# Giving VectorE's steps from a head pair's sums to their reciprocals a high scheduling rank in a masked attention kernel

## The chip, the cores and the metric

The kernel runs on one core of a Trainium2 chip. The metric is the device time of one execution in microseconds (us), the median of several runs. A profile is one more execution, taken by the hardware profiler.

## What is computed

The reference is one attention layer with a residual, over 16 batches of 1024 tokens with 512 channels and 8 heads of 64. The same projection serves as query, key and value. The mask is 0 or 1 per token.

```python
xt = jnp.transpose(x, (0, 2, 1))
q = xt @ Wq.T
qh = q.reshape(B, T, NH, dk).transpose(0, 2, 1, 3)
scores = scale * jnp.einsum('bhqd,bhkd->bhqk', qh, qh)
logits = (scores * cmask + (1.0 - cmask) * NEG) * rmask
attn = jax.nn.softmax(logits, axis=-1)
ctx = jnp.einsum('bhqk,bhkd->bhqd', attn, qh)
out = ctx.transpose(0, 2, 1, 3).reshape(B, T, D) @ Wo.T
return x + jnp.transpose(out, (0, 2, 1))
```

A token whose mask is 0 attends to every token alike, so its row of the result is a mean. About half of the tokens have mask 1.

## The kernel before, in words

The kernel gathers the tokens with mask 1 of a batch into 544 slots (C), 512 of them in four tiles of 128 and a tail of 32 (CT), and does the attention over these alone. The other tokens get the mean's projection, added by their own path (L798). Slots beyond the number of kept tokens hold the mean too; what they add to a softmax sum is worked out (corr, L571 and L572) and subtracted.

The work of one batch b goes through 18 steps, in a list S. A pair p is two heads (p is 0 to 3). For a pair and a tile i of 128 slots, `scores` computes the logits of both heads on TensorE (L620, into the two buffers of the psum pool pss), and ScalarE takes the exponential (L624), which also writes the sum over a row into z. Two further steps do the 32 slots of the tail for four heads at once, a group g (pairs 0 and 1 are group 0, pairs 2 and 3 group 1): the matmuls L595, the exponential L599 with its sums into zt, then on VectorE a split of the result into a high and a low part (L604 and L605), and four transfers on SP's queue that lay these parts out as pt (L611 from L604's result, L612 from L605's). Of pt, the first L611 and the first L612 serve the even pair of the group, the others the odd pair.

`attend` multiplies the exponentials by the values: 32 matmul records of L643 for a pair's tile, accumulating in pav, and four of L647 for the tail, which read pt. ScalarE copies pav out (L651).

The sums become reciprocals in `recip_sums`, the function that is changed. Its VectorE steps are: L666 subtracts corr from the eight sums z of a pair; L671 does the same for the tail's sums, once per head, between partitions of different groups (it reads zt and corr at partitions 32 q and writes partitions 0 to 31); L672 clamps and scales; L673 takes the reciprocal; L674 multiplies by the mask hit of valid slots. All write rcol, of which there are two tiles, one for even pairs and one for odd ones. Then `recip_rows` transposes rcol on TensorE (L680), copies ten rows out on VectorE (L683, which already has the high rank), sends them to memory and back spread over partitions (rd L685 and rb L688, on SP). `norm` multiplies the copied-out pav by rb (L711) and splits it for the output projection (L712 to L717), whose matmuls are L727 and whose eviction, with the residual, is L732. Its results go out with indirect transfers on GpSimd's queue (L811).

Between these steps stands the work for the next batches: gathering (L339), transposes (L424) and their splits (L384, L385), the query projection L447 with its eviction L450 and L453 and its split into hl (L461 to L463, then transfers into xx), the values (L497, L500, L484, L485), range checks (L392, needed only at the end), loads of 512 KB of x for the means (xm, L374), and the row maxima that bound the exponent: L541 and L543 gather squares into smcol, L549 transposes them on TensorE, L551 takes the maximum m, L558 spreads it on TensorE, and L560 to L563 make nm from it. All psum tiles but pss and pav come from the pool pm, of two buffers.

What sets the order: `run` lists the calls batch by batch, with a cost for each, and deals them out over the steps. A scheduler then orders the instructions of each engine. It takes them by rank, which is the place in the program; `high_priority(offset=HPO)`, with HPO = 300, moves the rank of what is issued inside it 300 places forward. Before the change it stands around the splits L384 and L385, the first L643 of a group, L683, L732 and the first row maxima. Each engine then executes its queue strictly in that order, with semaphores for what it needs from the others. `behind` and `once` add order by hand; L711 waits for TensorE's progress that way (for pairs 0 to 2).

Of the kernel before, what the change touches and what calls it, by code (L numbers as in the profile page):

```python
# [15 lines left out]
ALU = mybir.AluOpType  # L16
# [3 lines left out]
P = 128  # L20
# [11 lines left out]
CT = C - 512  # L32
# [3 lines left out]
HG = H // 2  # L36
# [6 lines left out]
SX = 256.0  # L43
# [3 lines left out]
HPO = 300  # L47


class Fast:  # L50
# [608 lines left out]
    def recip_sums(self, b, p):  # L659

        nc, s = self.nc, self.st[b]
        hs, g = slice(2 * p, 2 * p + 2), p // 2
        corr = s["corr"][g]
        r = self.rcol[p % 2][:, :10]
        m = r.rearrange("p (h k) -> p h k", k=5)
        nc.vector.tensor_tensor(m[:, :, :4], s["z"][:, hs, :],  # L666
                                corr[:, p % 2 * 2:p % 2 * 2 + 2].unsqueeze(2).broadcast_to([P, 2, 4]), ALU.subtract)
        for h in range(2):
            q = (2 * p + h) % HG
            rows = slice(q * CT, (q + 1) * CT)  # L670
            nc.vector.tensor_tensor(m[:CT, h, 4:5], s["zt"][rows, g:g + 1], corr[rows, HG:], ALU.subtract)  # L671
        nc.vector.tensor_scalar(r, r, 1e-35, 1.0 / SX, ALU.max, ALU.mult)  # L672
        nc.vector.reciprocal(r, r)  # L673
        nc.vector.tensor_tensor(m, m, self.hit[:, b, :].unsqueeze(1).broadcast_to([P, 2, 5]), ALU.mult)  # L674

    def recip_rows(self, b, p):

# [532 lines left out]
```

## Time and profile before

| | us |
|---|---|
| median of 3 runs | 1070.85 (1070.66 to 1076.17) |
| the profiled execution | 1064.91 |
| its span, first to last instruction | 1063.1 |
| TensorE busy (PE) | 1021.6 |
| VectorE busy (DVE) | 729.2 |
| ScalarE busy (ACT) | 672.5 |
| GpSimd busy (POOL) | 298.6 |
| the lines of recip_sums on VectorE, busy | 10.5 (L666), 19.0 (L671), 11.3 (L672), 13.5 (L673), 10.7 (L674) |
| TensorE idle before L680, waiting for L674 | 6.3, in 9 waits |

How to read it: PE is TensorE's matmuls and PEld its weight loads, which overlap them. The mean granted clock of TensorE was 0.992. A row of a timeline has the start in us, the duration of a run of equal instructions, engine, line, operation, result and operands, shape, and in brackets how long the engine had been idle and what ended that. A row of the view of waits has who waited, for whom, and then us in total, number of waits and the longest. Matmuls are pipelined: rows of them overlap, and one that takes 0.28 us holds the engine for about 0.12.

### The profile page before, as it was taken

Reading aid. Unit: us, or ns where it says so; the run is one execution under the profiler, and the core shown is the slowest. Engines: PE = TensorE matmul, PEld = TensorE weight load, DVE = VectorE, ACT = ScalarE, POOL = GpSimd, SP = SyncE. Lnnn points to the kernel's source line nnn. Section 1 sums busy time; section 2 is a strip of 40 time slices with the busy share of each in tenths; the row PEclk is TensorE's granted clock in tenths of the full one; section 3 lists DMA queues with packets and bytes.
Section 4 is the critical chain, followed back from the end, with each engine's and each line's share of the span. In section 5 each row is a group of like instructions: output and inputs, shape, how many; then the busy total and the mean of one; then the engine's idle time right before and its main releaser. Section 6 shows DMA issues by size and latency. Waiting matters only on the chain.

```text
span 1063.1 us, 23765 instructions
## 1 busy us (share of the span) xinstructions
PE 1021.6 (96%) x8626; PEld 701.6 (66%) x8626; DVE 729.2 (69%) x2376; ACT 672.5 (63%) x1722; POOL 298.6 (28%) x303
## 2 busy tenths in 40 slices
PE   7798999999999999999999999999999999999996
PEld 7576666666666767666676666767666676766553
DVE  6697668676766856776775766876676776666653
ACT  5876666666676766666676576676666676664550
POOL 3101013322301222332322223232232332235652
PEclk9899999999999999999999999999999999999998
DMA  6746555546654665766557575655856554575752
GB/s 206 226 132 166 136 166 165 177 142 204 174 145 137 160 189 156 195 194 165 173 149 210 167 199 172 162 166 148 239 174 179 170 159 144 142 195 170 222 172 76
DMA packets 78123, 181.37 MB, mean 171 GB/s; under 512 B 15008, under 2 KB 16800, under 8 KB 78000
## 3 DMA queue, kind: packets, MB, share of 16 engines
q1 hardware_dynamic: 56816, 111.62, 38.4%
q0 software_dynamic: 21184, 68.18, 20.5%
q8 instruction: 70, 1.15, 0.5%
q14 instruction: 53, 0.43, 0.1%
HBM read 92.34 MB, written 33.91 MB: 119 GB/s over the span
## 4 chain that ended last, share of the span: by engine, by line
PE 76%; ACT 10%; DVE 7%; issue 3%; DMA 2%; POOL 0%; POOLq 0%; DVEq 0%; SPq 0%; ACTq 0%
PE pav L643 22%; PE pss L620 17%; PE pm L727 15%; PE pm L447 12%; ACT p L624 5%; PE pm L424 2%; PE pav L647 2%; ACT xh L384 1%; DVE p L605 1%; ACT xm L369 1%; PE pss L595 1%; PE pm L497 1%; PE pm L680 1%; ACT v L500 1%; ACT p L599 1%
## 5 line engine op out<-in xcount | busy, mean ns | idle before, releaser
L624 ACT ACTIVATE p<-pss,nm 128x544 f32<-128x544 f32 x512 | 365.4, 718 | 217.5 <-PE pss L620 203.6
L620 PE MATMUL pss<-xx 128*128 128x272 f16 x2048 | 307.0, 280 | 6.5 <-ACT p L624 5.7
L643 PE MATMUL pav<-p,v 128*64 128x272 f32 x2048 | 248.8, 396 | 0.0
L620 PEld LDWEIGHTS <-xx 128*128 128x128 f16 x2048 | 194.7, 99 | 63.3 <-issue 22.5
L643 PEld LDWEIGHTS pav<-p,v 128*64 128x64 f32 x2048 | 141.4, 137 | 91.0 <-issue 13.9
L811 POOL DMA_INDIRECT y_out<-xa,idx x68 | 72.1, 1060 | 292.8 <-PE pss L620 150.2
L447 PE MATMUL pm<-xh,wqh 128*128 128x274 f16 (+1 forms) x512 | 143.9, 281 | 2.4 <-DVE xa L732 1.9
L447 PE MATMUL pm<-xh,wql 128*128 128x274 f16 (+1 forms) x512 | 143.2, 280 | 0.0
L447 PE MATMUL pm<-xl,wqh 128*128 128x274 f16 (+1 forms) x512 | 143.1, 280 | 0.0
L339 POOL DMA_INDIRECT xa<-x_in,idx x68 | 67.9, 999 | 210.6 <-PE pss L620 101.5
L447 PEld LDWEIGHTS <-wqh 128*128 128x128 f16 x1024 | 98.1, 99 | 25.8 <-issue 4.8
L624 ACT ACTIVATION_READ_ACCUMULATOR p<-pss,nm 128x1 f32 x512 | 104.0, 203 | 0.0
L811 POOL DMA_INDIRECT y_out<-xi,idx x60 | 69.5, 1159 | 107.5 <-PE pss L620 49.0
L727 PE MATMUL pm<-woh,ch 128*128 128x512 f16 x240 | 91.1, 380 | 0.0
L727 PE MATMUL pm<-woh,cl 128*128 128x512 f16 x240 | 90.9, 379 | 0.0
L727 PE MATMUL pm<-wol,ch 128*128 128x512 f16 x240 | 90.9, 379 | 0.0
L450 ACT ACTIVATE q<-pm 128x272 f32<-128x272 f32 (+1 forms) x128 | 50.9, 398 | 63.0 <-PE pm L447 62.8
L339 POOL DMA_INDIRECT xi<-x_in,idx x60 | 61.4, 1023 | 102.2 <-PE pss L620 43.5
L732 DVE SCALAR_TENSOR_TENSOR xa<-pm,xa 128x512 f32<-128x512 f32 x60 | 41.3, 688 | 63.3 <-PE pm L727 59.9
L727 PEld LDWEIGHTS <-ch 128*128 128x128 f16 x480 | 45.6, 98 | 45.9 <-issue 1.4
L798 DVE TENSOR_TENSOR xi<-xi,ub 128x512 f32<-128x512 f32 (+1 forms) x60 | 40.9, 688 | 42.6 <-PE pss L620 42.0
L711 DVE TENSOR_TENSOR c<-c,rb 128x544 f32<-128x544 f32 x64 | 46.2, 722 | 28.0 <-PE pm L447 17.1
(194 smaller groups left out, 1558.4 us busy)
## 6 DMA issues: line engine op xcount, KB each, us to landing
xx<-hl SPq DMA_DIRECT2D x256, 136.0 KB
xm<-x_nat_in SPq DMA_DIRECT2D x56, 512.0 KB
rb<-rd SPq DMA_DIRECT2D x128, 136.0 KB
pt<-c SPq DMA_DIRECT2D x64, 136.0 KB
pt<-p SPq DMA_DIRECT2D x64, 136.0 KB
ub<-ud SPq DMA_DIRECT2D x16, 256.0 KB
xi<-x_nat_in SPq DMA_DIRECT2D x8, 256.0 KB
xa<-x_in,idx POOLq DMA_INDIRECT x68, 4.6
```

The costliest lines, as they stand in the source:

```text
L339: dma = self.nc.gpsimd.indirect_dma_start(out=tile[:n], out_offset=None, in_=self.x, in_offset=bass.IndirectOffsetOnAxis(ap=idx, axis=0))
L424: self.pe = nc.tensor.transpose(pt[:, c, :], x[:n, c * P:(c + 1) * P], self.ident[:n, :n]).ins
L447: self.beat = nc.tensor.matmul(pq, lhsT=w[:, c, e * P:(e + 1) * P], rhs=xx[:, c, cols], start=(k == 0), stop=(k == 3 * DC - 1)).ins
L450: nc.scalar.activation(s["q"][:, e, cols], pq, AF.Copy, scale=1.0 / (SX * SW))
L620: self.beat = nc.tensor.matmul(pt[:, g, :CH], lhsT=xx[:, 2 * k, i * P:(i + 1) * P], rhs=xx[:, 2 * k + a, g * CH:(g + 1) * CH], start=(a == ...
L624: self.exp = [nc.scalar.activation(t.rearrange("p (g c) -> p g c", g=2), pt[:, :, :CH], AF.Exp, bias=s["nm"][p // HG][:, p % HG:p % HG + 1 ...
L643: mm = nc.tensor.matmul(s["pav"][k * DK:(k + 1) * DK, g, :CH], lhsT=s["v"][p][:, i, k * DK:(k + 1) * DK], rhs=ps[k][:, cols], start=(i == ...
L711: self.once(nc.vector.tensor_tensor(c, c, s["rb"][p], ALU.mult), self.beat if p < 3 else None)
L727: nc.tensor.matmul(po[:cols.stop - cols.start], lhsT=a[:, e, cols], rhs=w[:, e, :], start=(e == 0 and k == 0), stop=(e == DC - 1 and k == 2))
L732: self.nc.vector.scalar_tensor_tensor(x, po, 1.0 / (SX * SW), x, ALU.mult, ALU.add)
L798: self.once(self.nc.vector.tensor_tensor(x[:n], x[:n], s["ub"][:n], ALU.add), self.beat)
L811: dma = self.nc.gpsimd.indirect_dma_start(out=self.out, out_offset=bass.IndirectOffsetOnAxis(ap=idx, axis=0), in_=x, in_offset=None)
```

## The change

The body of `recip_sums` from the choice of rcol's tile on is put inside `with self.tc.high_priority(offset=HPO)`. No instruction, tile, shape or transfer is added or removed; the line numbers behind it grow by one.

```diff
@@ -661,17 +661,18 @@
         nc, s = self.nc, self.st[b]
         hs, g = slice(2 * p, 2 * p + 2), p // 2
         corr = s["corr"][g]
-        r = self.rcol[p % 2][:, :10]
-        m = r.rearrange("p (h k) -> p h k", k=5)
-        nc.vector.tensor_tensor(m[:, :, :4], s["z"][:, hs, :],
-                                corr[:, p % 2 * 2:p % 2 * 2 + 2].unsqueeze(2).broadcast_to([P, 2, 4]), ALU.subtract)
-        for h in range(2):
-            q = (2 * p + h) % HG
-            rows = slice(q * CT, (q + 1) * CT)
-            nc.vector.tensor_tensor(m[:CT, h, 4:5], s["zt"][rows, g:g + 1], corr[rows, HG:], ALU.subtract)
-        nc.vector.tensor_scalar(r, r, 1e-35, 1.0 / SX, ALU.max, ALU.mult)
-        nc.vector.reciprocal(r, r)
-        nc.vector.tensor_tensor(m, m, self.hit[:, b, :].unsqueeze(1).broadcast_to([P, 2, 5]), ALU.mult)
+        with self.tc.high_priority(offset=HPO):
+            r = self.rcol[p % 2][:, :10]
+            m = r.rearrange("p (h k) -> p h k", k=5)
+            nc.vector.tensor_tensor(m[:, :, :4], s["z"][:, hs, :],
+                                    corr[:, p % 2 * 2:p % 2 * 2 + 2].unsqueeze(2).broadcast_to([P, 2, 4]), ALU.subtract)
+            for h in range(2):
+                q = (2 * p + h) % HG
+                rows = slice(q * CT, (q + 1) * CT)
+                nc.vector.tensor_tensor(m[:CT, h, 4:5], s["zt"][rows, g:g + 1], corr[rows, HG:], ALU.subtract)
+            nc.vector.tensor_scalar(r, r, 1e-35, 1.0 / SX, ALU.max, ALU.mult)
+            nc.vector.reciprocal(r, r)
+            nc.vector.tensor_tensor(m, m, self.hit[:, b, :].unsqueeze(1).broadcast_to([P, 2, 5]), ALU.mult)
```

## The prediction, made before the changed kernel ran

> **What bounds the kernel.** I read the page first: TensorE is busy for 96% of the span and holds three quarters of the chain that ended last, and VectorE holds 7% of it.
>
> ```profile
> PE 1021.6 (96%) x8626; PEld 701.6 (66%) x8626; DVE 729.2 (69%) x2376; ACT 672.5 (63%) x1722; POOL 298.6 (28%) x303
> ...
> PE 76%; ACT 10%; DVE 7%; issue 3%; DMA 2%; POOL 0%; POOLq 0%; DVEq 0%; SPq 0%; ACTq 0%
> ```
>
> So an edit of VectorE's order counts only where TensorE stands idle for VectorE, or comes to. TensorE's queue is in order, so each such wait is paid in full. The view of waits, TensorE's own, has these rows (us in total, times, longest); its gaps over 0.06 us sum to 32.5 us, 10.8 of them in the first 41 us:
>
> ```profile
> PE pm L680 <- DVE rcol L674: 6.3, 9, 0.7
> PE pss L620 <- ACT p L624: 5.7, 13, 0.7
> ...
> PE pav L647 <- DMA pt<-p: 2.4, 1, 2.4
> ...
> PE pm L447 <- DVE xa L732: 1.9, 5, 0.4
> PE pm L558 <- DVE m L551: 1.1, 5, 0.2
> ...
> PE pm L680 <- ACT p L624: 0.7, 1, 0.7
> ```
>
> The chain of the change ends in the first and the last row: the transpose L680 waits ten times, always for pair 2, in batches 1, 3, 4, 6, 7, 9, 10, 12, 13 and 14. For the other 54 pairs L680 came 0.3 to 7.1 us after L674, or with no gap: there an earlier reciprocal buys nothing. **The most the change can remove is 6.9 us**, plus the 1.9 us of the L447 row if VectorE's eviction L732 came earlier.
>
> One such place on VectorE's timeline (start, us, ...), batch 3, and TensorE's wait at it:
>
> ```profile
> 272.18 0.48 DVE L604 CAST c<-p 128x544 fp32r<-128x544 f32 x1 [0.33 <-ACT p L599]
> 272.58 0.30 DVE L671 TENSOR_TENSOR rcol<-zt,corr 32x1 f32<-32x1 f32 x2
> 272.92 0.72 DVE L605 TENSOR_TENSOR p<-p,c 128x544 fp32r<-128x544 f32 x1
> 273.56 0.17 DVE L672 TENSOR_SCALAR rcol<-rcol 128x10 f32<-128x10 f32 x1
> 273.76 0.31 DVE L671 TENSOR_TENSOR rcol<-zt,corr 32x1 f32<-32x1 f32 x2
> 274.10 0.22 DVE L673 RECIPROCAL rcol<-rcol 128x10 f32<-128x10 f32 x1
> 274.35 0.17 DVE L674 TENSOR_TENSOR rcol<-rcol,hit 128x10 f32<-128x10 f32 x1
> ```
> ```profile
> 274.67 0.30 PE L680 MATMUL pm<-ident,rcol 128*128 128x128 f32 x1 [0.70 <-DVE rcol L674]
> ```
>
> The chain cannot start when the exponentials of the pair are done (269.18): L671 needs the tail's sums, which ScalarE's L599 delivers at 272.15, and L604 needs the same tile.
>
> **The change, part by part.** No instruction is added or removed. The rank goes to the scheduler that writes the queues, so I read the order of the built programs. GpSimd's is the same. 508 rows of VectorE's order move. TensorE's differs in 41 places, all small. On SP the transfers pt (from L604 and L605) and the 512 KB loads xm (L374) change places. Pitch of VectorE, from its timeline: an independent instruction starts 0.08 us before the one ahead ends, a dependent one 0.03 us after; L671 lasts 0.148 us, and what follows it starts 0.014 us after its end. So four L671 in a row hold the queue for 0.066 + 3 x 0.162 + 0.096 = 0.65 us (the first overlaps; the follower doesn't).
>
> A rule on this: the Trainium skill, "VectorE: DVE Perf Modes", section "Two Vector instructions with no wait between them", says an instruction is held until all earlier ones end when its input starts in another group of 32 partitions than the last one's. L671 reads a new group each time, so it speaks against pulling these steps forward; without it the four would take 0.27 us by the pitch of the other rows, and part 2 below would cost 1.3 us and not 3.1. The row decides, and it shows the hold.
>
> 1. *The ten waits.* New order in the nine batches: four L671, L672, L604, L673, L605, L674. The scheduler leaves L604 and L605 inside the chain. From 272.18: L671 to 272.83, L672 to 273.0, L604 from 272.9, L673 from 273.3, L605 from 273.4, L674 ends at 274.2 instead of 274.52. **Gain 9 x 0.31 = 2.8 us**, not 6.3: 0.4 us of each wait stays.
>
> 2. *Group 0 in batches 2, 5, 8, 11, 14.* There the four L671 (for pairs 0 and 1) now stand ahead of L485, where VectorE has no idle time until L551; before, they came some 7 us later and nobody waited. In batch 5:
>
> ```profile
> 359.55 0.68 DVE L485 TENSOR_REDUCE sd<-tmp 128x8 f32<-128x512 f32 x1
> 360.14 0.43 DVE L604 CAST c<-p 128x544 fp32r<-128x544 f32 x1
> ...
> 361.83 0.16 DVE L543 TENSOR_TENSOR smcol<-smcol,sdt 128x4 f32<-128x4 f32 x1
> ...
> 362.77 0.28 DVE L551 TENSOR_REDUCE m<-pm 128x1 f32<-128x128 f32 x1
> ```
> ```profile
> 362.24 0.27 PE L549 MATMUL pm<-ident,smcol 128*128 128x128 f32 x1
> ...
> 363.20 0.35 PE L558 MATMUL pm<-ident,m 128*128 128x4 f32 x2 [0.22 <-DVE m L551]
> ```
>
> L543 ended at 361.99, 0.25 us before L549; L558 waits for L551 already. A shift of 0.65 us goes through to L558 nearly whole. **Loss 5 x 0.62 = 3.1 us.** This is what is queued behind the new early steps, and TensorE waits for it.
>
> 3. *Group 0 in batches 3, 4, 6, 7, 9, 10, 12, 13.* Two L671 were ahead of L551 already, now four: L551 is 0.33 us later. L558 follows it directly (239.04 + 0.28, then 239.40). The new order of TensorE puts one matmul of L620 (0.12 us) ahead of L558. **Loss 8 x 0.21 = 1.7 us.**
>
> 4. *Group 1 in batches 2, 5, 8, 11.* L732 comes 0.43 us later, and TensorE's order now has the 32 matmuls of L643 (3.8 us) ahead of the L447 that waited 0.38 us for it: gain 4 x 0.38 = 1.5. L647 then stands 0.85 us earlier (0.38, and four L620 of 0.47 put behind it), and pt's first half landed 0.45, 1.6, 1.8 and 0.63 us ahead of it: new waits of 0.4 and 0.2 us. SP issues these pt late anyway (210.97, after xx), so L604's shift is hidden. **Gain 0.9 us.**
>
> 5. *Batch 14.* The chain and two hl steps now stand ahead of L543, which comes 2.1 us later, so L549 starts at 969.4 instead of 968.55. L680 moves ahead of twelve L447 and waits for the psum buffer that L551 frees, at about 971.75. From there: L447 1.4 us, L620 0.94, so L643 starts at 974.2 instead of 973.09; the two waits below are in that already. **Loss 1.1 us.**
>
> ```profile
> 969.73 0.28 PE L447 MATMUL pm<-xh,wqh 128*128 128x272 f16 x1 [0.45 <-DVE xa L732]
> ...
> 972.83 0.33 PE L680 MATMUL pm<-ident,rcol 128*128 128x128 f32 x1 [0.63 <-DVE rcol L674]
> ```
>
> 6. *Batch 0.* L605 ends 0.45 us later, and with it pt; TensorE waits for that pt already (2.39 us, at 88.60). **Loss 0.4 us.**
>
> 7. *SP.* In six batches (3, 6, 7, 9, 10, 12) xm is now issued ahead of pt. Cost between nothing and 2.4 us each (batch 0's wait, where xm went first too). I take nothing: in batch 4 xm went first already (335.16, pt from 335.79), pt's first half landed at 341.25 and L647 read it at 343.80, 2.5 us of cover; without that cover the delay would be paid whole. In eight batches xm is issued some 2 us later; ScalarE reads it much later, and no row shows ScalarE waiting for it.
>
> Sum: -2.8 + 3.1 + 1.7 - 0.9 + 1.1 + 0.4 = **+2.6 us** on the profiled execution (1064.91 us with a span of 1063.1), so 1067.5. That execution was 5.9 us under the median of the runs shown, 1070.85; carried over, **1073.5 us**. ScalarE is 0.3 to 0.7 us late at some L571 (it waits for L563), where TensorE is late by as much; I add nothing.
>
> **Rivals.** (A) *Faster:* the rank clears all ten waits and L732's: 6.9 + 1.9 = 8.8 us less, 1062. For it, the view of waits; against it, L604 and L605 still stand inside the chain, and parts 2 and 3. (B) *Slower, by pt:* at L647 of pair 2 in the six batches of part 7. Cover there was 1.7 to 4.2 us; PE arrives 0.3 us earlier and L605 is 0.45 us later, so a landing more than 0.9 to 3.4 us later decides. At batch 0's price, 6 x 2.4 = 14 us more: 1088, and half of it 1081. (C) *Nothing of note:* VectorE is off the path, the small shifts vanish in slack I misjudged: 1070.9. (D) *The losses stand, the gains don't* (the waits at L680 stay 0.7 because the psum buffer or ScalarE holds them): 2.6 + 3.7 gives 1077.
>
> **How the numbers follow.** Forecast 0.55, C 0.2, D 0.12, B 0.09, A 0.04. The measurement tells apart about 0.5% (5.4 us). Faster by more: A, 0.04. Slower by more: B, most of D, and the upper edge of the forecast, 0.2. The rest, 0.76, is within. The range takes in the forecast, C and D, with 3 to 4 us at either end for the spread of the runs (1070.66 to 1076.17), and leaves out A and most of B: 1067 to 1080.
>
> **What would show it.** The row L680 <- L674 at about 3.6 us in 9 waits of 0.4; the row L558 <- L551 up from 1.1 to about 5 (with some at L549 <- L543); no L447 <- L732; small new waits at L647 near 217 and 788; TensorE's gaps from 32.5 to about 35. Wrong if L680 doesn't wait at all, if L549 and L558 don't wait in group 0, or if L647 waits in the six batches.

## The result and the profile after

The changed kernel takes 1075.64 us (median of 20 runs, 1072.36 to 1079.56), the kernel before 1071.06 us beside it (20 runs, 1068.24 to 1076.17): a ratio of **1.0041, 95% interval 1.0032 to 1.0051**, so 4.6 us slower, where 1073.5 us, 2.6 more than before, was forecast. The profiled execution took 1075.52 us with a span of 1073.8. That is 10.6 us more than before's profiled one (1064.91), which was 6 us below its own median; the two traces differ by more than the change makes, and its share has to be told from the rest.

From L666 on, lines of the changed kernel are one higher: L680 is L681, L671 is L672, L674 is L675, L711 is L712, L727 is L728, L732 is L733. The page after, its busy times and its chain:

```profile
PE 1025.3 (95%) x8626; PEld 700.7 (65%) x8626; DVE 722.9 (67%) x2376; ACT 672.2 (63%) x1722; POOL 301.5 (28%) x303
...
PE 71%; DVE 11%; ACT 7%; DMA 5%; issue 4%; SPq 1%; POOL 0%; POOLq 0%; DVEq 0%; ACTq 0%
```

VectorE is busy 6 us less, and its share of the chain rises from 7% to 11%: it is not the amount of its work that counts but where TensorE waits for it. TensorE's waits after (us in total, times, longest):

```profile
PE pm L681 <- DVE rcol L675: 4.5, 9, 0.5
...
PE pav L647 <- DMA pt<-p: 3.3, 5, 1.1
...
PE pm L549 <- DVE smcol L543: 2.7, 6, 0.6
...
PE pm L447 <- DVE nm L560: 2.1, 3, 1.3
...
PE pm L558 <- DVE m L551: 1.8, 7, 0.6
```

The waits that the change is about have shrunk from 7.0 us in ten (6.3 in nine, and 0.7 in the row that the view puts down to ScalarE) to 4.5 us in nine. The row of L447 waiting for L732 is gone. New are 2.5 us at L549, 1.7 at L447 for nm (L560) and 0.7 at L558. For pt there are four new waits of 0.3 to 1.1 us, 2.6 in all, while the one of batch 0 is 0.7 us here and was 2.4 in before.

**How the time was placed.** I took the start of the same matmul in two traces and subtracted. From the transpose L680 of batch 1's pair 1 to that of batch 14's pair 3 (135.77 to 989.67 us in before) this difference changes only at a few matmuls, at most of them by the same amount in each profile; two profiles of before differ by 0.29 us over this stage, three of the changed kernel by 2.5. Outside of it the thirteen profiles differ by up to 8.5 us ahead of the stage and 4.9 behind it, and not in step with the change: no_tail comes to the stage 6.3 us later than before, cast_6_10 1.5 us earlier. Of the 10.7 us between the spans of after and before, 0.7 lie ahead of the stage, 8.1 in it and 1.9 behind it. The stage, in us against the first profile of before, split by the parts of the prediction (a minus is a gain; a2 and a3 are two more profiles of the changed kernel; the other columns are experiments told below):

| part | forecast | after | a2 | a3 | group0 | group1 | flat |
|---|---|---|---|---|---|---|---|
| 1, nine waits at L680 | -2.8 | -1.9 | -1.8 | -1.8 | 0 | -1.8 | -6.0 |
| 2, group 0, five batches | +3.1 | +3.9 | +3.9 | +3.9 | +3.9 | 0 | +1.7 |
| 3, group 0, eight batches | +1.7 | +4.4 | +4.2 | +4.4 | +4.0 | +0.1 | +1.1 |
| 4, group 1, batches 2, 5, 8, 11 | -0.9 | +0.1 | -1.1 | -1.2 | 0 | -0.8 | -0.4 |
| 5, batch 14 | +1.1 | +0.6 | -0.1 | -0.1 | +0.2 | -0.1 | -0.7 |
| 7, pt in batch 3 | 0 | +1.1 | +0.6 | +0.6 | 0 | 0 | +1.5 |
| whole stage | +2.2 | +8.1 | +5.7 | +5.6 | +8.0 | -1.7 | -2.9 |

(Part 6, 0.4 us in batch 0, lies ahead of the stage, where the scatter hides it. The rows are rounded and leave out up to 0.9 us at other matmuls, most of it group1's 0.74 in batch 2.) The three profiles of the changed kernel agree to 0.2 us in parts 1, 2 and 3; nearly all their disagreement is in parts 4, 5 and 7, at waits for transfers.

### The profile page after: what moved, and what is told of

It reads as the page before. It is cut to its first block, busy times and chain, and to the rows that moved or that the text cites. A ratio compares the mean times of both kernels' runs of the same rounds, so it can differ in the third digit from the quotient of the medians.

```text
span 1073.8 us, 23792 instructions
## 1 busy us (share of the span) xinstructions
PE 1025.3 (95%) x8626; PEld 700.7 (65%) x8626; DVE 722.9 (67%) x2376; ACT 672.2 (63%) x1722; POOL 301.5 (28%) x303
## 4 chain that ended last, share of the span: by engine, by line
PE 71%; DVE 11%; ACT 7%; DMA 5%; issue 4%; SPq 1%; POOL 0%; POOLq 0%; DVEq 0%; ACTq 0%
PE pav L643 20%; PE pss L620 16%; PE pm L728 15%; PE pm L447 10%; ACT p L624 3%; DMA pt<-p 2%; PE pav L647 2%; DMA xx<-hl 2%; PE pm L424 2%; ACT xh L384 2%; DVE top L392 2%; DVE sd L485 1%; DVE rcol L672 1%; DVE tmp L484 1%; PE pm L497 1%
## 5 line engine op out<-in xcount | busy, mean ns | idle before, releaser
L620 PE MATMUL pss<-xx 128*128 128x272 f16 x2048 | 306.8, 279 | 6.4 <-ACT p L624 3.0
L620 PEld LDWEIGHTS <-xx 128*128 128x128 f16 x2048 | 194.4, 99 | 66.6 <-issue 25.7
L812 POOL DMA_INDIRECT y_out<-xa,idx x68 | 73.2, 1077 | 299.7 <-PE pss L620 147.7
L447 PE MATMUL pm<-xh,wqh 128*128 128x274 f16 (+1 forms) x512 | 143.6, 280 | 2.4 <-DVE nm L560 2.1
L447 PE MATMUL pm<-xl,wqh 128*128 128x274 f16 (+1 forms) x512 | 143.0, 279 | 0.2 <-DVE xl L385 0.2
L447 PE MATMUL pm<-xh,wql 128*128 128x274 f16 (+1 forms) x512 | 142.9, 279 | 0.0
L447 PEld LDWEIGHTS <-wqh 128*128 128x128 f16 x1024 | 97.6, 99 | 26.8 <-issue 6.0
L339 POOL DMA_INDIRECT xi<-x_in,idx x60 | 64.9, 1081 | 106.4 <-PE pss L620 59.5
L728 PE MATMUL pm<-woh,ch 128*128 128x512 f16 x240 | 91.1, 380 | 0.0
L728 PE MATMUL pm<-woh,cl 128*128 128x512 f16 x240 | 90.9, 379 | 0.0
L728 PE MATMUL pm<-wol,ch 128*128 128x512 f16 x240 | 90.9, 379 | 0.0
L733 DVE SCALAR_TENSOR_TENSOR xa<-pm,xa 128x512 f32<-128x512 f32 x60 | 41.3, 689 | 63.1 <-PE pm L728 58.9
L712 DVE TENSOR_TENSOR c<-c,rb 128x544 f32<-128x544 f32 x64 | 46.1, 721 | 48.9 <-PE pm L447 28.6
L728 PEld LDWEIGHTS <-ch 128*128 128x128 f16 x480 | 45.6, 98 | 45.9 <-issue 1.3
```

The source lines that it names most:

```text
L339: dma = self.nc.gpsimd.indirect_dma_start(out=tile[:n], out_offset=None, in_=self.x, in_offset=bass.IndirectOffsetOnAxis(ap=idx, axis=0))
L447: self.beat = nc.tensor.matmul(pq, lhsT=w[:, c, e * P:(e + 1) * P], rhs=xx[:, c, cols], start=(k == 0), stop=(k == 3 * DC - 1)).ins
L620: self.beat = nc.tensor.matmul(pt[:, g, :CH], lhsT=xx[:, 2 * k, i * P:(i + 1) * P], rhs=xx[:, 2 * k + a, g * CH:(g + 1) * CH], start=(a == ...
L712: self.once(nc.vector.tensor_tensor(c, c, s["rb"][p], ALU.mult), self.beat if p < 3 else None)
L728: nc.tensor.matmul(po[:cols.stop - cols.start], lhsT=a[:, e, cols], rhs=w[:, e, :], start=(e == 0 and k == 0), stop=(e == DC - 1 and k == 2))
L733: self.nc.vector.scalar_tensor_tensor(x, po, 1.0 / (SX * SW), x, ALU.mult, ALU.add)
```

## The experiments

Times are medians; "before" is its median beside the same runs.

| run | time | before | ratio, 95% interval | stage |
|---|---|---|---|---|
| a2 (the change again) | 1074.22 | 1071.13 | 1.0035 [1.0022, 1.0048] | +5.7 |
| group0 | 1081.23 | 1071.13 | 1.0089 [1.0069, 1.0109] | +8.0 |
| group1 | 1068.53 | 1071.13 | 0.9971 [0.9957, 0.9986] | -1.7 |
| no_tail | 1071.40 | 1071.13 | 1.0007 [0.9994, 1.0020] | +0.8 |
| flat | 1060.51 | 1064.07 | 0.9960 [0.9943, 0.9977] | -2.9 |
| a3 (the change again) | 1076.25 | 1071.68 | 1.0041 [1.0024, 1.0057] | +5.6 |
| cast_6_10 | 1076.73 | 1071.68 | 1.0039 [1.0023, 1.0054] | +5.2 |
| b2 (before again) | 1065.82 | 1064.07 | 1.0010 [0.9995, 1.0024] | +0.3 |
| nine | 1064.46 | 1064.07 | 1.0001 [0.9985, 1.0017] | +0.5 |
| nine_clear | 1059.32 | 1064.07 | 0.9944 [0.9925, 0.9963] | -5.6 |
| eleven | 1065.11 | 1071.68 | 0.9936 [0.9913, 0.9959] | -5.4 |

My theory: the loss is made by pairs 0 and 1 and the gain by pairs 2 and 3, and what makes both is L671, which takes a place in VectorE's queue and holds it. Rivals: the transfers of pairs 2 and 3 carry the loss; or any reordering of VectorE of this size costs something.

### The rank for half of the pairs

group0, and group1 with `p >= 2`:

```diff
-        with self.tc.high_priority(offset=HPO):
+        with (self.tc.high_priority(offset=HPO) if p < 2 else ExitStack()):
```

> The rank for pairs 0 and 1 alone (p < 2). My theory: this carries the whole loss, parts 2 and 3 of the prediction, read from the trace after as 3.3 + 2.8 = 6.1 us; so 6 us slower than before (1077, ratio 1.0057; 1.003 at least), with L549 and L558 waiting in group 0 and the ten waits at L680 unchanged at 0.7. Rival (the loss came from the transfers pt and xm and from batch 14, all in pairs 2 and 3): no change, ratio within 0.001 of 1.

> The rank for pairs 2 and 3 alone (p >= 2). My theory: the gains with what goes with them, -1.9 (L680 waits 0.5 instead of 0.7 in nine batches), +0.2 (part 4), -0.3 (batch 14), +1 (one late pt): 1 us faster, 1070, ratio 0.999 (0.997 to 1.0005); no wait at L549 in batches 2, 5, 8, 11 and L558 waits as before, 1.1 us in 5. Rival (the transfers carry the loss): 4 to 5 us slower, ratio 1.004, with waits at L647 for pt in two batches or more.

The two halves part as my theory says: group0 alone is slower by 0.89%, group1 alone faster by 0.29%. group0 costs 8.0 us in the stage, 1.9 more than expected, and nothing of it comes at L680, whose nine waits are 0.70 to 0.71. Its waits:

```profile
PE pm L549 <- DVE smcol L543: 2.9, 7, 0.6
...
PE pm L447 <- DVE nm L560: 1.7, 3, 0.8
```

group1's, where neither L549 nor nm has grown over before:

```profile
PE pm L681 <- DVE rcol L675: 4.5, 9, 0.5
...
PE pm L549 <- DVE smcol L543: 0.4, 2, 0.2
PE pm L447 <- DVE nm L560: 0.4, 1, 0.4
```

Group0's and group1's stages sum to +6.2, the changed kernel's are +5.6 to +8.1: nothing new is seen to come from having both. **The kernel with the rank for pairs 2 and 3 alone beats before.**

### The rank on everything but L671

```diff
                 rows = slice(q * CT, (q + 1) * CT)
-                nc.vector.tensor_tensor(m[:CT, h, 4:5], ...)
+                with self.tc.high_priority(offset=-HPO):
+                    nc.vector.tensor_tensor(m[:CT, h, 4:5], ...)
```

> The changed kernel with the rank taken off the two L671 of each pair (the rest of the chain keeps it). The order of TensorE's and SP's work is that of before, VectorE's differs at some 500 places. My theory: L671, which waits for the tail's sums and holds the queue, alone carries both the losses and the gain, so nothing changes: ratio 1.000 (0.999 to 1.001), L680 waits 0.7 in nine batches, no wait at L549 for L543. Rival (any reordering of VectorE of this size costs some us): ratio 1.002 or more.

1.0007 with 1 inside the interval. From batch 3 to batch 14 the start of every milestone (L549, L680) is within 0.1 us of before's after the common shift, though 660 of the 2376 places of VectorE's queue hold another instruction. The 0.8 of the stage is a wait of L558 for n (L196) in batch 2, which group1 and eleven show too and the three profiles of the changed kernel do not. It is not the order's: nine_clear has the same order as eleven up to there and does not wait. This reordering costs nothing by itself. The gain is gone as well, so it is L671's place in the queue that carries both.

### L671 without its hold

```diff
-                rows = slice(q * CT, (q + 1) * CT)
-                nc.vector.tensor_tensor(m[:CT, h, 4:5], ..., corr[rows, HG:], ALU.subtract)
+                rows = slice(0, CT)
+                nc.vector.tensor_tensor(m[:CT, h, 4:5], ..., corr[rows, HG:], ALU.is_ge)
```

> The changed kernel, with L671 reading the same 32 partitions of the tail's sums for all heads and giving the outcome of a comparison instead of the difference (so the last 32 rows are normalised by other numbers; the queues are the same). Theory: the loss is made by the hold of L671, 0.096 us each where it reads another group of partitions; without it four in a row take 0.27 us and not 0.65. L549 and L558 then wait about 0.36 us less in each of the five batches 2, 5, 8, 11, 14, 0.2 less in the eight others, and L680 0.2 less in nine: 4 to 6 us under the changed kernel, ratio to before 0.9995 (0.998 to 1.0015). Rival (a small instruction costs 0.16 us whatever it reads): ratio 1.0035 as for the changed kernel.

The queues are the changed kernel's. VectorE in batch 5 of the changed kernel (a2), start, us, and the same place in flat:

```profile
361.22 0.64 DVE L672 TENSOR_TENSOR rcol<-zt,corr 32x1 f32<-32x1 f32 x4
361.89 0.69 DVE L485 TENSOR_REDUCE sd<-tmp 128x8 f32<-128x512 f32 x1
...
364.18 0.15 DVE L543 TENSOR_TENSOR smcol<-smcol,sdt 128x4 f32<-128x4 f32 x1
```
```profile
357.81 0.36 DVE L672 TENSOR_TENSOR rcol<-zt,corr 32x1 f32<-32x1 f32 x4
358.10 0.67 DVE L485 TENSOR_REDUCE sd<-tmp 128x8 f32<-128x512 f32 x1
...
360.38 0.14 DVE L543 TENSOR_TENSOR smcol<-smcol,sdt 128x4 f32<-128x4 f32 x1
```

From the first L672 to the start of L485 it is 0.67 us with four different groups of 32 partitions and 0.29 with one: 0.38 us of hold, four times 0.096. L671 itself is hardly shorter (0.141 us, 0.148 in a2), so it is not the other operation that saves the time: the next one starts 0.07 us after it instead of 0.16. TensorE's loss in these batches falls from 0.74 to 0.34 each. In six of the eight batches of part 3 the loss of 0.37 becomes a gain of 0.09, and the nine waits at L680 vanish: 0.67 each against before, 0.47 more than the changed kernel gains, where I had expected 0.2 more. So flat is faster than before by 0.40%, not level with it: I was right on the mechanism and had the last place too small, since without the hold the chain ends 1.67 us after its release in batch 3 (270.37 to 272.04) against 2.15 in a2 and 2.34 in before. This is the rule that the prediction weighed (the Trainium skill, "VectorE: DVE Perf Modes", section "Two Vector instructions with no wait between them"), and the runs agree with it, at 0.1 us per instruction. The +1.1 us that flat keeps in part 3 come from batch 10 alone (+1.65), and are another wait, for nm: the next section. flat normalises the last rows wrongly, so it is a measurement and no version to use.

### Waits for nm in batches 6 and 10

I had read these two waits of the first profile as scatter:

> The changed kernel again, to part what recurs from what scattered. My theory (the time is made of small shifts of VectorE's order): 1075.6 us, ratio 1.004 to before; TensorE's waits at the transpose of smcol for L543 again about 2.7 us in 6, at the transpose of rcol for the reciprocals about 4.5 us in 9 with 0.5 the longest. The two waits of L447 for nm (0.34 and 1.30 us, batches 6 and 10) and the late start of batch 15 (2.7 us) have no reason in the order, so I expect them gone or at other places. Rival (they belong to the change): the same waits in the same batches, 1 us or more together.

> The changed kernel a third time, beside the run above and on the same chip. Theory: ratio 1.0035 to 1.0045; the waits of L447 for nm again in batches 6 and 10; from the middle of batch 1 to the end of batch 14 5.5 to 8 us more than before (two profiles gave 8.1 and 5.7, the difference lying in three waits for pt in batches 3, 8 and 11 and one for rb in batch 10). Rival (what differs between those two profiles is not the landing of transfers): other places differ.

They recur: 0.49 and 0.92 us in a2, 0.54 and 1.11 in a3, 0.44 and 0.79 in group0, in these batches none in before, b2, group1 or no_tail. My expectation for a2 was wrong there; the late start of batch 15 is another thing (told with b2). SP's queue around batch 6 in a2 (start, us), and VectorE's:

```profile
425.20 0.30 SPq L686 DMA_DIRECT2D rd<-rr  x1
428.18 0.46 SPq L611 DMA_DIRECT2D pt<-c  x1
428.74 1.19 SPq L689 DMA_DIRECT2D rb<-rd  x2
```
```profile
434.49 0.73 DVE L712 TENSOR_TENSOR c<-c,rb 128x544 f32<-128x544 f32 x1 [1.51 <-DMA rb<-rd]
...
438.15 0.15 DVE L560 TENSOR_SCALAR nm<-pm 128x4 f32<-128x4 f32 x1
```

The same place on SP's queue in before:

```profile
423.25 0.31 SPq L685 DMA_DIRECT2D rd<-rr  x1
424.73 1.10 SPq L611 DMA_DIRECT2D pt<-c  x2
425.92 1.19 SPq L688 DMA_DIRECT2D rb<-rd  x2
```

The first pt needs L604, which now stands behind four L671 and L485. It holds SP's queue: 2.98 us from rd to pt, 1.48 in before. rb stands behind it; L712 needs rb and stands idle at the head of VectorE's queue for 1.51 us, and L560, whose nm TensorE's L447 waits for, is behind L712. Of the steps in which the rank moves group 0's L671, only those of batches 6 and 10 have L560 behind L711, in before too. To test that it is this path and not a backlog of VectorE, only L604 and L605 of group 0 (p is the group here) in batches 6 and 10 were put first again:

```diff
-            nc.vector.tensor_copy(hi, t)
-            nc.vector.tensor_tensor(lo, t, hi.bitcast(F32), ALU.subtract)
+            with (self.tc.high_priority(offset=HPO) if p == 0 and b in (6, 10) else ExitStack()):
+                nc.vector.tensor_copy(hi, t)
+                nc.vector.tensor_tensor(lo, t, hi.bitcast(F32), ALU.subtract)
```

> The changed kernel; only in batches 6 and 10 L604 and L605 of group 0 get the high rank too and stand ahead of L485 again, so that on SP the first pt no longer holds back rb; TensorE's order is that of the changed kernel. In these two batches VectorE's L543 is later by another 0.5 us for it. Theory (the waits of L447 for nm there, 0.34 to 0.49 and 0.9 to 1.3 us, come by SP: L604 late, so pt late, so rb behind it late, and L560 queued behind the L711 that waits for rb): both waits for nm vanish, against 0.3 to 0.4 us more at L549 in each: 0.5 to 1 us less than the changed kernel, ratio to before 1.003. Rival (L560 is late because VectorE has a backlog): the waits for nm stay or grow by the 0.5 us, and VectorE's wait for rb stays.

Its SP queue at the same place, and VectorE's L712 (here L713):

```profile
423.55 0.30 SPq L687 DMA_DIRECT2D rd<-rr  x1
424.95 1.10 SPq L612 DMA_DIRECT2D pt<-c  x2
426.14 1.20 SPq L690 DMA_DIRECT2D rb<-rd  x2
```
```profile
431.28 0.72 DVE L713 TENSOR_TENSOR c<-c,rb 128x544 f32<-128x544 f32 x1
```

Both waits for nm are gone, though VectorE's L543 is later there and L549 pays for it: 0.84 and 0.71 us instead of 0.19. Batch 6 costs 0.57 instead of 0.60 to 0.81 and batch 10 0.45 instead of 1.2 to 1.6. So the late L604 and the order on SP make the wait, and a backlog of VectorE does not. In the time the gain cannot be told (1.0039 beside 1.0041 for a3); the two batches gain 0.9 to 1.2 us, and waits for pt at other places leave 0.4 to 0.5 of that in the stage against a2 and a3.

Not all of the path is shown. In batch 6 of a2 rb is issued 3.54 us after rd and in before 2.67, 0.9 us later, but L712 starts 9.29 us after rd where L711 started at 7.02. Over half of the delay thus lies between the issue of rb and its landing, and no run tells why. In flat rb is issued 3.07 us after rd in both batches; in batch 6 TensorE does not wait for nm, in batch 10 L712 stands idle for 2.88 us and TensorE waits 1.35.

### Before again

No edit.

> The kernel before again, for a second profile of it. From batch 1 to batch 14 the four changed kernels' traces agree with before to 0.02 us wherever the order is the same, while the first 120 us and the first third of batch 15 differ by 2 to 6 us whatever the kernel. Theory: these two places scatter from execution to execution, and the first profile of before was lucky in both; so the span between the first pair-2 transpose of batch 1 and the last transpose of batch 14 repeats within 1 us (742.75 us in the first profile), and batch 15 shows a wait of 2.5 to 3.1 us at L620 that the first profile lacks. Rival (the reordering causes that wait): it is missing again. Ratio 1.000.

The stage repeats to 0.29 us, as expected (from the first pair-2 transpose of batch 1 on it was 842.76 us in the first profile; the 742.75 above is a slip). The wait in batch 15 was not there, as in the first profile of before. It was not in nine, nine_clear or flat either, and flat has the changed kernel's queues, so it does not follow the order. The profiles that show it (2.6 to 3.2 us in a2, group0, group1, no_tail, cast_6_10 and eleven; smaller in after and a3) come from other sets of runs. Each set had a chip of its own: flat, b2, nine and nine_clear ran on one (14 in the record), where before takes 1064 us, a2, group0, group1 and no_tail on a second (5) and a3, cast_6_10 and eleven on a third (10), where before takes 1071 to 1072. The first profile of before, at 1064.91 us, lies under all 67 executions of before in the other sets (1067.96 at least). So the wait goes with the chip or the set, not with the change, and a ratio is good only against the before beside it. In a2 ScalarE stands idle for 3.48 us ahead of L780, with nothing in the profile that it waits for, in b2 (there L779) for 1.40. Why stays open.

The wait for n in batch 2 divides the same way: the three kernels that leave group 0 as it was in batch 2 have it on chips 5 and 10 (group1, no_tail and eleven, 0.74 to 0.77 us), and none has it on chip 14. Before was not profiled on chips 5 and 10. If it waits there too, up to 0.74 of the 0.89 us that part 2 counts in batch 2, and of the stage, is not the change's.

### Versions that take the gain alone

Only pair 2 of the nine batches (run nine):

```diff
-        with self.tc.high_priority(offset=HPO):
+        with (self.tc.high_priority(offset=HPO) if p == 2 and b % 3 != 2 and 0 < b < self.B - 1 else ExitStack()):
```

> The rank only for pair 2 of the nine batches 1, 3, 4, 6, 7, 9, 10, 12, 13. TensorE's and SP's order is that of before, and VectorE's differs around these nine places only. Theory: the nine waits at L680 fall from 0.70 to 0.50 and nothing else moves: -1.8 us, ratio 0.998 (0.997 to 0.9995). Rival (pt, from the L604 and L605 that now stand behind four L671, comes late for L647): 1.000 or more, with waits at L647.

No gain: 1.0001. VectorE in nine, batch 3:

```profile
270.00 0.35 DVE L672 TENSOR_TENSOR rcol<-zt,corr 32x1 f32<-32x1 f32 x2 [0.33 <-ACT p L599]
270.38 0.44 DVE L604 CAST c<-p 128x544 fp32r<-128x544 f32 x1
270.74 0.20 DVE L673 TENSOR_SCALAR rcol<-rcol 128x10 f32<-128x10 f32 x1
270.97 0.15 DVE L672 TENSOR_TENSOR rcol<-zt,corr 32x1 f32<-32x1 f32 x1
271.15 0.73 DVE L605 TENSOR_TENSOR p<-p,c 128x544 fp32r<-128x544 f32 x1
271.79 0.21 DVE L674 RECIPROCAL rcol<-rcol 128x10 f32<-128x10 f32 x1
272.03 0.15 DVE L672 TENSOR_TENSOR rcol<-zt,corr 32x1 f32<-32x1 f32 x1
272.21 0.17 DVE L675 TENSOR_TENSOR rcol<-rcol,hit 128x10 f32<-128x10 f32 x1
```

The chain ends 2.38 us after its release at 270.00; in before it was 2.34. Pair 3's two L671 have no rank here and still get in between, each with its hold on both sides, and L604 and L605 too. My theory held that pair 2's place alone makes the gain; it does not. The waits at L647 that the rival expected are not there either.

So in nine_clear the steps in between were moved: besides the edit above, L604 and L605 of group 1 in these batches (put into a function `cast`) are issued after L674, and their transfers pt (`spread`) right behind them. The part of the edit that does it:

```diff
+        if p == 2 and "cast" in s:
+            cast, spread = s.pop("cast")
+            with self.behind(end):
+                cast()
+            spread()
```

> As in the kernel with the nine places, and L604 and L605 of that step are put behind the whole chain, so that the reciprocals come some 0.9 us earlier than before. On SP the 512 KB load xm now goes ahead of pt in six of the nine batches. Theory: the nine waits at L680 are gone (-6.3), pt comes about 1 us later, for which 1.7 to 4.2 us of cover were read: -5 to -6.3 us, ratio 0.995 (0.994 to 0.997). Rival (what was behind the wait is late next: ScalarE's buffers at L620, or pt behind xm at 2.4 us each in six batches): gain under 2 us, ratio 0.998 or more, with waits at L620 for L624 or at L647 for pt in its place.

Faster by 0.56%: this beats both kernels. VectorE in batch 3:

```profile
271.07 0.69 DVE L677 TENSOR_TENSOR rcol<-zt,corr 32x1 f32<-32x1 f32 x4 [0.33 <-ACT p L599]
271.79 0.22 DVE L678 TENSOR_SCALAR rcol<-rcol 128x10 f32<-128x10 f32 x1
272.04 0.22 DVE L679 RECIPROCAL rcol<-rcol 128x10 f32<-128x10 f32 x1
272.29 0.17 DVE L680 TENSOR_TENSOR rcol<-rcol,hit 128x10 f32<-128x10 f32 x1
272.38 0.44 DVE L604 CAST c<-p 128x544 fp32r<-128x544 f32 x1
```

The chain ends 1.39 us after its release. L680 gains 0.80 us in each of the nine, 7.2 in all, and 1.6 is given back, 0.45 of it by pt in batch 3. Though xm goes ahead of pt on SP in six of the nine batches, as in the changed kernel, no other place gives back more than 0.27 us: the rival's 2.4 us each are not there.

Last, with the rank for pair 2 in batches 5 and 8 too (`b in (1, 3, 4, 5, 6, 7, 8, 9, 10, 12, 13)`):

> The kernel with the nine places cleared, and the rank for pair 2 in batches 5 and 8 too, where the run with pairs 2 and 3 alone gained 0.52 and 0.53 us (there L447 no longer waits 0.37 for L732). Theory: 1 us under the kernel with the nine places, ratio to before 0.9935 (0.992 to 0.9955). Rival (L647's new waits for pt take it back, as in two of the three profiles of batch 8 in the changed kernel): ratio 0.9945 or more.

0.9936, and 0.52 us less in each of the two batches, as expected. Beside nine_clear (0.9944) the intervals overlap, and in the stage a late pt in batch 3 (1.2 us, 0.45 there) and L558's wait for n in batch 2 take the 1 us back: the order of the two is not settled.

## Why the prediction came out as it did

The sign and the range were right, and the sum was too small: 2.2 us for the stage against 5.6 to 8.1. The median moved by 4.6 us (3.1 and 4.6 in the other two comparisons), less than the stage; what makes up the difference stays open: the first 120 us and batch 15, which scatter by more, lie outside of it, and the wait for n in batch 2 may be part of it. That the total came within 2.1 us of 1073.5 is in part luck: a loss that did not come (part 5, 1.1 us) hides most of a wait that was not foreseen (1.2 to 1.4 us).

- **Part 1, the ten waits.** The order was read rightly, and that most of each wait stays. The gain is 0.20 us each, not 0.31 (0.26 in batch 1). In batch 3 of a2 four L671 took 0.69 us, not 0.65, L605 started 1.29 us after the release and L674 ended at 2.15, where 2.02 was worked out.
- **Part 2.** Right: 0.62 forecast, 0.74 measured (0.89 in batch 2), 3.9 us for 3.1. The prediction had the shift arrive at L558; 0.63 of it comes at L549 already, and another 0.11 at L558. flat shows that the hold is half of it (0.40 of 0.74).
- **Part 3 is the term that failed.** "L551 is 0.33 us later. L558 follows it directly", less 0.12: 0.21 each. Measured 0.37. I looked at L551 alone; all four L671 now stand ahead of L485 there too, L543 ends about 0.8 us later, and L549, which had started 0.76 us after it, is 0.19 late as well. L558 then adds 0.18: L551 is 0.49 late, not 0.33. That is 3.0 us instead of 1.7. Batch 3 in before and in a2, whose start is 0.63 us later by then:

```profile
237.16 0.15 DVE L543 TENSOR_TENSOR smcol<-smcol,sdt 128x4 f32<-128x4 f32 x1
238.07 0.27 PE L549 MATMUL pm<-ident,smcol 128*128 128x128 f32 x1
239.40 0.36 PE L558 MATMUL pm<-ident,m 128*128 128x4 f32 x2
```
```profile
238.59 0.15 DVE L543 TENSOR_TENSOR smcol<-smcol,sdt 128x4 f32<-128x4 f32 x1
238.89 0.30 PE L549 MATMUL pm<-ident,smcol 128*128 128x128 f32 x1
240.49 0.38 PE L558 MATMUL pm<-ident,m 128*128 128x4 f32 x2 [0.18 <-DVE m L551]
```

- **What was missing** is the wait for nm in batches 6 and 10, 1.2 to 1.4 us of part 3. Part 4 had said of SP's pt that L604's shift was hidden, and part 7 asked only what xm does to pt. Neither asked what stands behind a pt whose L604 is late. That was the step to add: a late producer holds SP's queue, and rb, behind it, is issued 0.9 us later and is on the path.
- **Part 4.** -0.9 forecast, -1.1 and -1.2 in two profiles and +0.1 in the third. The waits for L732 are gone and pt decides: 0.5 us of gain where it is in time, 0.7 of loss where it is not (batch 8 of after).
- **Part 5.** Wrong: no loss of 1.1 but -0.1 (+0.6 in after, where L497 waits 0.71 for xx). L549 is 0.70 us late where 0.85 was worked out. The transpose L680 does not stand ahead of the twelve L447, as the prediction read the order: in a2 it starts at 977.90, behind the last of them (977.73), and has moved ahead of eight L620 alone. It waits for no psum buffer: no gap of TensorE's stands there. The waits of 0.45 and 0.63 us that before had are replaced by 0.52 (L549) and 0.16 (L447).
- **Part 6** cannot be told: the wait for pt in batch 0, 2.39 us in the first profile, is 0.83 in the second one of before and between nothing and 3.3 us in the others. So 2.4 us was no price to multiply in rival B either.
- **Part 7.** Right in five of six batches; batch 3's pt is 0.55 to 1.05 us late in all three profiles. Rival B did not come.
- **Rivals.** A is out: L680 kept 0.5 of each wait. C is out: the stage of the changed kernel is 5.6 to 8.1 us longer where before repeats to 0.29. D gave 1077 for another reason: the gains stand, the losses are larger.
- **The signs.** The waits in group 0 came, but mostly at L549 (2.7 us) and not at L558 (1.8, where about 5 was named); the row of L680 is 4.5 us in nine and not 3.6; TensorE's gaps sum to 36 to 39 us and not 35.

## What to carry to other kernels

A rank moves an instruction ahead of others in a queue that is in order, so price what it is put ahead of, at every place where it applies and not only where the wait was seen: here nine waits asked for it and 64 places got it. Give it only there, and check that the whole chain moves, since one step left behind (L604 and L605, pair 3's L671) holds the rest. Then follow each delayed instruction one queue further: what it feeds may be the head of a DMA queue that something on the path stands in, as the first pt stood ahead of rb here.

## What the runs showed of the hardware

- An L671 that reads another group of 32 partitions than the one ahead costs 0.096 us more than one that reads the same: four and their follower take 0.67 us against 0.29. Ahead of L485, where VectorE has no idle time, TensorE sees it whole (0.40 us a batch for 0.38).
- Most of VectorE's order is worth nothing to TensorE here: with another instruction at 660 places of VectorE's queue and L671 left in place, TensorE's milestones from batch 3 to 14 came within 0.1 us of before's.
- Two profiles of before repeat to 0.3 us over 850 us in the middle; three of the changed kernel differ by 2.5 us there, at waits for transfers, and agree to 0.2 us at the waits for VectorE that parts 1 to 3 count. A change of 0.4% is better read from such a stage, wait by wait, than from two whole spans, which differed here by 10.7 us.
- The same kernel, before, took 1064 us on one chip and 1071 to 1072 on two others (medians of 23 to 29 runs).
